# A message-passing layer on one core: the edge stage taken two groups at a time, with its PSUM banks shared out anew

## The chip, the cores and the metric

The kernel runs on one core of a Trainium2 chip. The metric is the device time of one execution in microseconds. TensorE (PE) does the matrix products and the transposes, VectorE (DVE) and ScalarE (ACT) read their results out of PSUM, GpSimd (POOL) issues the gathers, and SyncE (SP) issues most of the plain transfers. PSUM has eight banks of 2 KB a partition.

## The reference

One layer of a graph network on 6250 nodes of 128 features and 100000 edges, sorted by destination, and then a residual sum and a layer norm. Everything is float32.

```python
msg_in = concat([x[src], x[dst]], -1)                 # 100000 x 256
h = relu(msg_in @ Wm1 + bm1)                          # 256
h = relu(h @ Wm2 + bm2)                               # 256
messages = h @ Wm3 + bm3                              # 128
agg = segment_sum(messages, dst) / clip(count, 1)
upd = relu(concat([x, agg], -1) @ Wn1 + bn1) @ Wn2 + bn2
out = layernorm(x + (x + upd))
```

## The kernel before

**Tables.** The first product is taken on the nodes instead of on the edges: a table `atab` holds x @ Wm1[:128] (float32), a table `btab` holds x @ Wm1[128:] split into three bfloat16 terms. An edge's first layer is then one row of `atab` by its source plus one row of `btab` by its destination. The third product is moved behind the sum over edges.

**Groups.** The edges are taken in 196 groups of 512 (`NG`, `GE`; the last group is half filled), each of four tiles of 128 edges (`GT`). Because edges are sorted by destination, a tile's destinations lie in a window of at most 21 nodes (`WB`; a dynamic loop behind the main one, empty for these inputs, takes what lies further).

**A group's way.** `fetch` gathers four times 128 rows of `atab` by an indirect DMA from POOL (L431) and copies four windows of `btab` by plain DMAs from SP (L437), into one of four buffers `rows`. `hot` makes one-hot matrices of the destinations on DVE (L452, L455). `first_layer` transposes the gathered rows on PE (L468, 16 products) and adds the `btab` terms by one-hot products (L474, 8 products of bfloat16) into `ph`, two banks, of which there is one; ACT takes the two relu out of it (L478). `second_layer` multiplies by Wm2 (L487, 16 products as the profile counts them) into two tiles `ph2` of one bank each, and DVE takes the bias and the relu out (L489). `sums` multiplies by a one-hot matrix to sum over a window's edges (L495, 8 products of 32 columns, four beside each other in the array) into `pg`, one bank, and ACT copies it out as `part` (L502). `add_up` transposes `part` on PE (L511, 6 products) into `pt`, two banks, and DVE adds its four windows to `acc` in SBUF (L516), at columns whose numbers DVE loads into registers (`load_bases`, L519).

**PSUM.** `p1` has `ph` (2 banks), `p2` two `ph2` (2), `pa` the `pg` (1), `ptp` the `pt` (2): seven banks.

**Order.** The stages of several groups are interleaved by hand. PE's order is fixed by a manual schedule. An iteration of the main loop gives PE

```python
sums(g-3); add_up(g-4) transposes; first_layer(g); second_layer(g-1)
```

The fetch of group g+2 is issued in the same iteration. The orders of DVE and ACT are by hand in the first six iterations and at the end, and are the scheduler's in between. Each of the first two groups has one node block's x @ Wn1 (`x_part`) with it; two more such blocks stand at the end of the loop. Every eighth iteration `double` loads a block of x, doubles it on DVE and stores it for the node stage.

**Before and after.** Ahead of the loop stands the making of the tables, behind it the node stage (L678 on): the third product, the node network and the norm.

Of the kernel before, what the change touches and what calls it, by code (L numbers as in the profile page):

```python
# [19 lines left out]
P = 128  # L20
# [7 lines left out]
def kernel(  # L28
# [109 lines left out]
    w1 = const.tile([P, 2, H], F32, name="w1")  # L138
# [12 lines left out]
    with tc.tile_pool(name="prep", bufs=1) as prep, tc.tile_pool(  # L151
# [3 lines left out]
    ) as pb:  # L155
        src_i = prep.tile([R, 2 * GE], I32, name="src_i", tag="src_i")
# [256 lines left out]
    with edge, tc.tile_pool(name="wk", bufs=2) as wk, tc.tile_pool(  # L413
        name="p1", bufs=1, space=PSUM
    ) as p1, tc.tile_pool(name="p2", bufs=2, space=PSUM) as p2, tc.tile_pool(
        name="pa", bufs=1, space=PSUM
    ) as pa, tc.tile_pool(name="pt", bufs=1, space=PSUM) as ptp:


        NH2 = 4  # L420
# [4 lines left out]
        def fetch(idx, nt, firsts):  # L425


            rows = ld.tile([P, (GT + 1) * H], F32, name="rows", bufs=4)
            ag = rows[:, :GT * H].rearrange("p (j h) -> p j h", j=GT)
            for j in range(GT):  # L430
                nc.gpsimd.indirect_dma_start(  # L431
                    out=ag[:, j, :], out_offset=None, in_=atab[:, :],
                    in_offset=bass.IndirectOffsetOnAxis(ap=idx[:, j:j + 1], axis=0))
            bw = rows[:, GT * H:].bitcast(BF16).rearrange("p (k h) -> p k h", k=2)
            for j, first in enumerate(firsts):
                terms = btab[ds(first, WB + 1)].rearrange("n c h -> (n c) h")
                nc.sync.dma_start(bw[j // 2 * NQ:(j // 2 + 1) * NQ, j % 2, :], terms[:NQ])  # L437
            return ag, bw
# [7 lines left out]
        def hot(db, pb_cols, dl, nt):  # L446


            n = nt * WN
            oht = wk.tile([P, 2, P], BF16, name="oht")  # L450
            for k in range(2):
                nc.vector.tensor_scalar(oht[:n, k, :], db[:n, k * P:(k + 1) * P], pb_cols[:n, k:k + 1], None,  # L452
                                        op0=ALU.is_equal)
            oh = wk.tile([P, GT, WN], F32, name="oh", bufs=4)
            nc.vector.tensor_tensor(oh[:, :nt, :], iota_n.to_broadcast([P, nt, WN]),  # L455
                                    dl.rearrange("p (j o) -> p j o", o=1).to_broadcast([P, nt, WN]),
                                    op=ALU.is_equal)
            return oht, oh
# [3 lines left out]
        def first_layer(ag, bw, oht, nt):  # L462
            nh = nt // 2
            ph = p1.tile([P, 2, HC, 2 * P], F32, name="ph")
            for c in range(HC):
                for u in range(GT):
                    for h in range(nh):
                        nc.tensor.matmul(ph[:, h, c, u * NQ:(u + 1) * NQ], ag[halves[h], u, c * P:(c + 1) * P],  # L468
                                         ident[halves[h], halves[h]], is_transpose=True,
                                         start=(c == 0 and u == 0), stop=False, skip_group_check=True)  # L470
            for c in range(HC):
                for k in range(2):
                    for h in range(nh):
                        nc.tensor.matmul(ph[:, h, c, k * P:(k + 1) * P], bw[halves[h], k, c * P:(c + 1) * P],  # L474
                                         oht[halves[h], k, :], start=False, stop=True, skip_group_check=True)
            h1 = wk.tile([P, HC, GE], F32, name="h1")
            for c in range(HC):
                nc.scalar.activation(h1[:, c, :nh * 2 * P].rearrange("p (h e) -> p h e", h=nh), ph[:, :nh, c, :],  # L478
                                     AF.Relu, bias=b1[:, c:c + 1])
            return h1  # L480

        def second_layer(h1, h2, nt):
            for j0 in range(0, nt, 2):
                ph2 = p2.tile([P, 2, H], F32, name="ph2")
                for a in range(2):
                    for c in range(HC):
                        nc.tensor.matmul(ph2[:, a, :], h1[:, c, (j0 + a) * P:(j0 + a + 1) * P],  # L487
                                         w2[:, c, :], start=(c == 0), stop=(c == HC - 1))
                nc.vector.tensor_tensor(h2[:, j0:j0 + 2, :H], ph2, nb2.to_broadcast([P, 2, H]), op=ALU.max)  # L489

        def sums(oh, h2, nt):

            pg = pa.tile([P, H + 1], F32, name="pg")
            for j in range(nt):
                nc.tensor.matmul(pg[j * WN:(j + 1) * WN, :], oh[:, j, :], h2[:, j, :],  # L495
                                 start=True, stop=True, skip_group_check=True)
            return pg

        def part_of(pg, nt):
            n = nt * WN  # L500
            part = wk.tile([P, H + 1], F32, name="part")
            nc.scalar.copy(part[:n, :], pg[:n, :])  # L502
            return part

        def add_up(part, firsts, nt):
            pt = ptp.tile([P, 2, 4 * P], F32, name="pt")[:, :, :(HC + 1) * NQ]
            pt = pt.rearrange("p h (c q) -> p h c q", q=NQ)
            for c in range(HC + 1):
                for h in range(nt // 2):
                    rows = part[halves[h], c * P:(c + 1) * P] if c < HC else part[halves[h], H:].to_broadcast([NQ, P])  # L510
                    nc.tensor.matmul(pt[:, h, c, :], rows, ident[halves[h], halves[h]], is_transpose=True,  # L511
                                     start=True, stop=True, skip_group_check=True)
            for j in reversed(range(nt)):
                window = acc[:, :, ds(firsts[j], WB)]
                k = j % 2 * WN
                nc.vector.tensor_add(window, window, pt[:, j // 2, :, k:k + WB])  # L516
# [28 lines left out]
        def bank_p1():  # L545
            return p1.tile([P, 2, HC, 2 * P], F32, name="ph")[:, 0]

        def bank_p2():
            return p2.tile([P, 2, H], F32, name="ph2")

        ahead, lag = 2, 3
        st, hots = {}, {}
        first = list(X_FIRST)
        for i in range(NG + ahead + 1):
            if i == 6:
                turns.close()
            if i == 16:
                late_loads()

                none = wk.tile([16, (NG * GE - E) // 16 + 1], I32, name="none", bufs=1)  # L560
                nc.vector.memset(none, NONE)
                nc.sync.dma_start(dpad[E - 16:].rearrange("(p e) -> p e", p=16), none)
                nc.sync.dma_start(dpad[:E].rearrange("(p e) -> p e", p=16), dst.rearrange("(p e) -> p e", p=16))
            for step, after in enumerate((20, 24, 27)):
                if i >= after and (i - after) % 8 == 0 and (i - after) // 8 < len(pieces):
                    double((i - after) // 8, step)
            if i < NG:
                nt = GT if i < NGF else LT
                firsts = load_bases(tilei[0:1, i * GT:(i + 1) * GT], nt, ENG.SP)
                if i == NGF:  # L570
                    dbs = last_destinations()
                elif i % 2 == 0:
                    dbs = early.pop(0) if early else destinations(i, min(2, NGF - i), dst_row)
                st[i] = dict(nt=nt, got=fetch(srcT[:, i, :], nt, firsts), db=dbs.pop(0))
            g = i - ahead
            if 0 <= g < NG:
                s = st[g]
                ag, bw = s.pop("got")

                def make_hot(g):  # L580
                    s = st[g]
                    hots[g], s["oh"] = hot(s.pop("db"), pbase[:, g, :], dloc[:, g, :s["nt"]], s["nt"])

                if g not in hots:
                    make_hot(g)
                oht = hots.pop(g)
            k = g - lag
            pg = sums(st[k]["oh"], st[k]["h2"], st[k]["nt"]) if 0 <= k < NG else None
            k = g - lag - 1
            if 0 <= k < NG:  # L590
                s = st.pop(k)
                if "firsts" not in s:
                    s["firsts"] = load_bases(tilei[0:1, k * GT:(k + 1) * GT], s["nt"], ENG.DVE)
                add_up(s["part"], s["firsts"], s["nt"])
            if 0 <= g < NG:
                s = st[g]
                s["h1"] = first_layer(ag, bw, oht, s["nt"])
            if pg is not None:
                st[g - lag]["part"] = part_of(pg, st[g - lag]["nt"])
# [220 lines left out]
```

## Time and profile before

| | |
|---|---|
| median of three runs | 1203.84 us (1203.38 to 1206.65) |
| the profiled execution | 1204.24 us |
| its span, first to last instruction | 1202.5 us |
| PE busy | 1180.1 us, 98% |
| PE weight loads busy | 896.9 us, 75% |
| POOL busy | 801.2 us, 67% |
| DVE busy | 675.7 us, 56% |
| ACT busy | 419.2 us, 35% |
| granted PE clock | 0.996 |
| gathers (L431) | 784, 955 ns each |

The profiled execution lies 0.4 us above the median, and its time is 1.7 us longer than its span. In the profile's rows a matmul's duration counts from its start to the end of its last result, so that the durations of neighbours overlap; what a stage takes is read from the start of its first product to the start of the next stage's first product.

### The profile page before, as it was taken

Reading aid. Unit: us, or ns where it says so; the run is one execution under the profiler, and the core shown is the slowest. Engines: PE = TensorE matmul, PEld = TensorE weight load, DVE = VectorE, ACT = ScalarE, POOL = GpSimd, SP = SyncE. Lnnn points to the kernel's source line nnn. Section 1 sums busy time; section 2 is a strip of 40 time slices with the busy share of each in tenths; the row PEclk is TensorE's granted clock in tenths of the full one; section 3 lists DMA queues with packets and bytes.
Section 4 is the critical chain, followed back from the end, with each engine's and each line's share of the span. In section 5 each row is a group of like instructions: output and inputs, shape, how many; then the busy total and the mean of one; then the engine's idle time right before and its main releaser. Section 6 shows DMA issues by size and latency. Waiting matters only on the chain. (4 is left out here: it accounts for less than half of the span.)

```text
span 1202.5 us, 32806 instructions
## 1 busy us (share of the span) xinstructions
PE 1180.1 (98%) x11196; PEld 896.9 (75%) x11197; DVE 675.7 (56%) x2077; ACT 419.2 (35%) x776; POOL 801.2 (67%) x862
## 2 busy tenths in 40 slices
PE   8999999999999999999999999999999999999997
PEld 6747777777777777777777777777777777777565
DVE  5764555555555455555555555555555555555587
ACT  5753332332332333233233323323323332332256
POOL 6567777777777777777777777777777777773120
PEclk9999999999999999999999999999999999999998
DMA  8886666676555555555555555555555555552243
GB/s 274 280 264 191 183 194 185 182 193 185 160 151 153 150 148 153 152 151 152 152 149 147 153 153 152 153 150 149 148 154 154 150 152 151 147 147 67 83 117 114
DMA packets 173733, 193.66 MB, mean 161 GB/s; under 512 B 30906, under 2 KB 145548, under 8 KB 173548
## 3 DMA queue, kind: packets, MB, share of 16 engines
q0 software_dynamic: 38160, 103.75, 31.5%
q1 hardware_dynamic: 106956, 61.93, 17.7%
q10 hardware_dynamic: 28448, 25.87, 7.3%
q8 instruction: 89, 1.46, 0.5%
q14 instruction: 80, 0.66, 0.2%
HBM read 168.92 MB, written 22.88 MB: 160 GB/s over the span
## 5 line engine op out<-in xcount | busy, mean ns | idle before, releaser
L431 POOL DMA_INDIRECT rows<-atab,srcT x784 | 749.0, 955 | 285.4 <-issue 181.0
L487 PE MATMUL ph<-w,h 128*128 128x256 f32 x3128 | 727.6, 386 | 0.1
L487 PEld LDWEIGHTS ph<-w,h 128*128 128x128 f32 x3128 | 579.0, 190 | 91.1 <-ACT x_sb L329 0.9
L489 DVE TENSOR_TENSOR h<-ph,nb 128x512 f32<-128x512 f32 x391 | 270.6, 693 | 388.7 <-PE ph L487 376.4
L478 ACT ACTIVATE h<-ph,b 128x512 f32<-128x512 f32 x392 | 247.3, 682 | 138.4 <-PE ph L474 133.1
L502 ACT COPY part<-pg 128x257 f32<-128x257 f32 x196 | 73.6, 376 | 575.5 <-PE pg L495 510.6
L516 DVE TENSOR_TENSOR acc<-acc,pt 128x63 f32 x782 | 172.0, 220 | 78.1 <-PE pt L511 20.5
L468 PE MATMUL ph<-ident,rows 64*128 64x64 f32 x3128 | 129.9, 223 | 1.3 <-ACT h L478 0.7
L495 PE MATMUL pg<-h,oh 128*32 128x257 f32 x1564 | 125.6, 392 | 0.0
L468 PEld LDWEIGHTS ph<-ident,rows 64*128 64x128 f32 x3128 | 113.1, 140 | 2.3 <-ACT h L478 0.9
L511 PEld LDWEIGHTS pt<-ident,part 64*128 64x128 f32 x1173 | 51.1, 137 | 81.5 <-issue 81.1
L452 DVE TENSOR_SCALAR oht<-db,pbase 128x128 bf16<-128x128 int32 x392 | 100.9, 289 | 0.1
L495 PEld LDWEIGHTS pg<-h,oh 128*32 128x32 f32 x1564 | 30.9, 108 | 65.8 <-issue 65.0
L511 PE MATMUL pt<-ident,part 64*128 64x64 f32 x1173 | 77.8, 239 | 0.1
L474 PE MATMUL ph<-oht,rows 64*128 64x128 bf16 x1564 | 76.1, 216 | 0.9 <-DMA rows<-btab 0.8
L701 POOL TENSOR_TENSOR agg<-total,rc 128x512 f32<-128x512 f32 (+2 forms) x15 | 16.0, 1069 | 69.5 <-DMA rcol<-acc 33.2
L455 DVE TENSOR_TENSOR oh<-iota_n,dloc 128x128 f32<-128x128 f32 x196 | 55.9, 285 | 0.0
L474 PEld LDWEIGHTS <-rows 64*128 64x128 bf16 x1564 | 53.2, 96 | 1.4 <-DMA rows<-btab 0.9
L235 PE MATMUL pbt<-w,xT 128*128 128x256 f32 x196 | 49.8, 398 | 3.9 <-DVE rest L255 1.2
L235 PEld LDWEIGHTS pbt<-w,xT 128*128 128x128 f32 x196 | 36.6, 198 | 13.4 <-DVE rest L255 2.9
L724 PEld LDWEIGHTS pot<-wu,u 128*128 128x128 f32 (+1 forms) x196 | 24.0, 191 | 5.1 <-issue 4.5
L696 PE MATMUL pmt<-acc,w 128*128 128x512 f32 (+2 forms) x60 | 24.8, 551 | 2.3 <-DVE rc L690 2.3
(111 smaller groups left out, 410.7 us busy)
## 6 DMA issues: line engine op xcount, KB each, us to landing
rows<-btab SPq DMA_DIRECT2D x782, 32.0 KB
db<-in_dst_dram ACTq DMA_DIRECT2D x194, 128.0 KB
rows<-atab,srcT POOLq DMA_INDIRECT x784
btab<-bt SPq DMA_DIRECT2D x24, 384.0 KB
atab<-bt SPq DMA_DIRECT2D x24, 256.0 KB
xd<-in_x_dram SPq DMA_DIRECT2D x12, 256.0 KB
x2tab<-xd SPq DMA_DIRECT2D x12, 256.0 KB
x_sb<-in_x_dram SPq DMA_DIRECT2D x5, 512.0 KB
```

The costliest lines, as they stand in the source:

```text
L235: nc.tensor.matmul(pbt[:, a, :], xT[:, (t0 + a) * P:(t0 + a + 1) * P], w1[:, k, :], start=True, stop=True)
L431: nc.gpsimd.indirect_dma_start(out=ag[:, j, :], out_offset=None, in_=atab[:, :], in_offset=bass.IndirectOffsetOnAxis(ap=idx[:, j:j + 1], a ...
L452: nc.vector.tensor_scalar(oht[:n, k, :], db[:n, k * P:(k + 1) * P], pb_cols[:n, k:k + 1], None, op0=ALU.is_equal)
L468: nc.tensor.matmul(ph[:, h, c, u * NQ:(u + 1) * NQ], ag[halves[h], u, c * P:(c + 1) * P], ident[halves[h], halves[h]], is_transpose=True, ...
L474: nc.tensor.matmul(ph[:, h, c, k * P:(k + 1) * P], bw[halves[h], k, c * P:(c + 1) * P], oht[halves[h], k, :], start=False, stop=True, skip ...
L478: nc.scalar.activation(h1[:, c, :nh * 2 * P].rearrange("p (h e) -> p h e", h=nh), ph[:, :nh, c, :], AF.Relu, bias=b1[:, c:c + 1])
L487: nc.tensor.matmul(ph2[:, a, :], h1[:, c, (j0 + a) * P:(j0 + a + 1) * P], w2[:, c, :], start=(c == 0), stop=(c == HC - 1))
L489: nc.vector.tensor_tensor(h2[:, j0:j0 + 2, :H], ph2, nb2.to_broadcast([P, 2, H]), op=ALU.max)
L495: nc.tensor.matmul(pg[j * WN:(j + 1) * WN, :], oh[:, j, :], h2[:, j, :], start=True, stop=True, skip_group_check=True)
L502: nc.scalar.copy(part[:n, :], pg[:n, :])
L511: nc.tensor.matmul(pt[:, h, c, :], rows, ident[halves[h], halves[h]], is_transpose=True, start=True, stop=True, skip_group_check=True)
L516: nc.vector.tensor_add(window, window, pt[:, j // 2, :, k:k + WB])
```

## The change

Every step of the edge stage takes a pair of groups in place of one: 98 iterations in place of 196.

- `first_layer` does the 32 transposes of both groups, then the 16 one-hot products of both; `ph` has four banks.
- `sums` stands behind the one-hot products, no longer at the head of the iteration, and sums both groups into a tile of two banks. PE's order in an iteration is now: the 12 transposes of `turned` (pair p-3), `first_layer` (pair p), `sums` (pair p-2), `second_layer` (pair p-1, first and second group).
- The results of `sums`, of `turned` and of the two `second_layer` calls, and of the `x_part` calls in the loop and behind it, all take turns in one pool of two tiles of two banks each (`banks`).
- `second_layer` takes a group's result out in one DVE instruction of 1024 columns for the first group and in two of 512 for the second (`cuts`).
- `part_of` copies both groups' sums in one ACT instruction.
- `rows` has two buffers, each for a pair. `h2s` has two tiles in place of four, `h1` is twice as large, `w1` moves into a pool that is closed after the tables.
- The loads of a pair's window columns on DVE stand ahead of its eight additions, and DVE's and ACT's orders are by hand throughout.

```diff
-        NH2 = 4
+        NH2 = 2
+        def banks():
+            return p2.tile([P, 2, 2 * H], F32, name="banks")
...
-            rows = ld.tile([P, (GT + 1) * H], F32, name="rows", bufs=4)
+            rows = ld.tile([P, 2, (GT + 1) * H], F32, name="rows", bufs=2)
...
-                oh = wk.tile([P, GT, WN], F32, name="oh", bufs=4)
+                oh = wk.tile([P, GT, WN], F32, name="oh", bufs=6)
...
-            ph = p1.tile([P, 2, HC, 2 * P], F32, name="ph")
+            ph = p1.tile([P, 2, 2, HC, 2 * P], F32, name="ph")
+            for i, ((ag, bw), nt) in enumerate(zip(got, nts)):
...
+            for i in reversed(range(len(nts))):
...
-        def second_layer(h1, h2, nt):
-            for j0 in range(0, nt, 2):
-                ph2 = p2.tile([P, 2, H], F32, name="ph2")
+        def second_layer(h1, h2, nt, cuts):
+            ph2 = banks().rearrange("p b (t h) -> p (b t) h", t=2)
             for j in range(nt):
+                for c in range(HC):
+                    nc.tensor.matmul(ph2[:, j, :], h1[:, c, j * P:(j + 1) * P],
+                                     w2[:, c, :], start=(c == 0), stop=(c == HC - 1))
+            step = nt // cuts
+            for j in range(0, nt, step):
+                nc.vector.tensor_tensor(h2[:, j:j + step, :H], ph2[:, j:j + step],
+                                        nb2.to_broadcast([P, step, H]), op=ALU.max)
+        def sums(groups):
+            pg = banks()
...
+        def turned(part, nts):
+            pt = banks()[:, :, :2 * (HC + 1) * NQ].rearrange("p h (g c q) -> p h g c q", g=2, q=NQ)
...
+        def add_up(pt, firsts, nts):
+            for i in reversed(range(len(nts))):
+                for j in reversed(range(nts[i])):
+                    window = acc[:, :, ds(firsts[i][j], WB)]
+                    k = j % 2 * WN
+                    nc.vector.tensor_add(window, window, pt[:, j // 2, i, :, k:k + WB])
+                    yield
...
+        for i in range(NP + 4):
...
+            if i < NP:
...
+            p = i - 1
+            k = p - 3
+            firsts = bases(k, ENG.DVE) if k >= 0 else None
+            if k >= 0:
+                pt = turned(st[k]["part"], st[k]["nts"])
+                whole(add_up(pt, firsts, st.pop(k)["nts"]))
...
+            if p + 1 < NP:
+                make_hot(p + 1)
+            if p < NP:
+                s["h1"] = first_layer(s.pop("got"), s.pop("ohts"), s["nts"])
+            if p < 2:
+                whole(x_part(X_FIRST[p], bank, (nc.scalar, nc.vector)))
+            if p - 2 == NP - 1:
+                whole(rest)
+            if 0 <= p - 2 < NP:
+                st[p - 2]["part"] = part_of(summed(p - 2), st[p - 2]["nts"])
+            if 0 <= p - 1 < NP:
+                for j, nt in enumerate(s["nts"]):
+                    second_layer(s["h1"][:, j], h2s[j], nt, 1 + j)
```

## The prediction

> **What bounds the kernel now.** I read the page first. PE is busy in 98% of the span, and the page's 40 slices show it at 9 tenths from the second to the last but one. So only less PE time, or a wait that displaces it, can move the end. A busy PE is not a PE at its peak, so I then read PE's timeline over one group in mid-run, where the stages repeat every 5.27 us:
>
> ```profile
> 604.79 0.64 PE L495 MATMUL pg<-h,oh 128*32 128x257 f32 x8
> 605.36 0.40 PE L511 MATMUL pt<-ident,part 64*128 64x64 f32 x6
> 605.60 0.66 PE L468 MATMUL ph<-ident,rows 64*128 64x64 f32 x16
> 606.10 0.39 PE L474 MATMUL ph<-oht,rows 64*128 64x128 bf16 x8
> 606.41 3.72 PE L487 MATMUL ph<-w,h 128*128 128x256 f32 x16
> 610.06 0.64 PE L495 MATMUL pg<-h,oh 128*32 128x257 f32 x8
> ...
> 147.63 2.64 PE L487 MATMUL ph<-w,h 128*128 128x256 f32 x11
> ```
>
> Columns: start, length, then the group. The starts give what each stage takes to the next one's first product: sums 0.57, turned sums 0.24, transposes 0.50, one-hot 0.31, second layer 3.65. The last line, cut off by the end of the query, gives the pace inside a stage: five products more (3.72 against 2.64) cost 1.08, 0.216 each. Sixteen at that pace are 3.46, so 0.19 of the 3.65 is paid once per visit. The tile view shows where half of it is: the first product runs 0.10 longer than the others (maximum against median):
>
> ```profile
> L487 PE MATMUL ph<-w,h x20: 378/379/483, 603.8 to 609.8; 128*128 128x256 f32 x20
> ```
>
> The same reading elsewhere: transposes (0.66 - 0.223)/7 = 0.062 a pair of products, eight pairs 0.50, nothing paid at entry; turned sums, three pairs 0.19, so 0.05 paid; one-hot (0.39 - 0.216)/3 = 0.057 a pair, four pairs 0.23, so 0.08 paid; sums, two rounds of four beside each other, 0.43, so 0.14 paid. **A group pays 0.19 + 0.05 + 0.08 + 0.14 = 0.47 us for entering and leaving stages.** No idle row shows it.
>
> Next, the timeline of the other engines, for what lies closest behind PE:
>
> ```profile
> 604.90 0.69 DVE L489 TENSOR_TENSOR h<-ph,nb 128x512 f32<-128x512 f32 x1 [1.03 <-PE ph L487]
> 605.51 0.28 DVE L455 TENSOR_TENSOR oh<-iota_n,dloc 128x128 f32<-128x128 f32 x1
> 606.12 0.98 DVE L516 TENSOR_TENSOR acc<-acc,pt 128x63 f32 x4 [0.33 <-issue]
> 606.59 1.26 ACT L478 ACTIVATE h<-ph,b 128x512 f32<-128x512 f32 x2 [0.66 <-PE ph L474]
> ...
> 98.84 0.95 POOL L431 DMA_INDIRECT rows<-atab,srcT  x1 [0.30 <-PE ph L487]
> 100.10 1.12 POOL L431 DMA_INDIRECT rows<-atab,srcT  x1 [0.30 <-issue]
> ```
>
> POOL's gathers follow each other at 1.257 us (98.84 to 100.10) when nothing holds them: 5.03 a group, only 0.24 below PE's 5.27. **POOL is the wall behind PE.**
>
> **The change part by part.** *Fewer stage visits.* A pair visits each stage once, so the 0.47 is paid once and not twice: the products of a pair take 2 x 5.27 - 0.47 = 10.08 us in place of 10.55. Here a rule bears: the Trainium skill's "TensorEngine Tiling (Array Packing)", Key Properties, says that a changed tiling mode drains TensorE, and "TensorE: Matmul & The Clock Gate", step by step, puts a drain at some 128 cycles, an estimated 0.05 us at its 2.4 GHz. A pair has three changes of tile shape fewer (64x128 to 128x128, to 128x32, back), so the rule's sum is 0.16 a pair, 15 us in all; the trace's is 0.47, 44 us. The trace has both sides of the gap, the drain and the first weights' load that nothing hides (the 0.10 above), so I take the trace.
>
> *Sums moved behind the one-hot products.* Sixteen products, same count. They wait for the last relu of the pair's second layer on DVE (over 0.8 us after that layer's end, by the L489 rows: last product at 604.49, DVE 604.90 to 605.59); sums come 1.95 into the iteration. Hidden.
>
> *Two tiles of two banks for all.* Turn by turn, `pt` and the first `ph2` share one, `pg` and the second `ph2` the other. So the first `second_layer` of an iteration waits for the eight additions on DVE, which had banks of their own. Count from the iteration's first product. PE wants that tile at 0.05 + 6 x 0.062 + 16 x 0.062 + 8 x 0.057 + 0.08 + 4 x 0.216 + 0.14, which is 2.96. DVE ends the last relu of the layer before at 0.80. The column load started as soon as the instruction ahead of it had gone out, and the additions 0.61 after that (605.51 to 606.12); a second load for the second group, 0.34 more, is an estimate from the length of such a load in the trace. Counted from the last relu's start (0.11), the first addition is at 1.06, the eighth seven steps of 0.255 later, its end at 3.07, PE's release some 0.06 after: 3.13. **PE stands 0.17 us in every pair.** A bound below: if both loads are hidden, additions start at 0.80 and end at 2.81, no wait. Above: if a load costs twice that, 0.5. A rule speaks against the change here: "Perfetto Trace Analysis", Optimizing Tensor Performance, wants independent products to rotate through different PSUM banks, so that one's reading overlaps the next one's writing. By the rows its price is the 0.17; without the rows it could be the whole of the additions. The second `ph2` wants its tile at 6.5 and gets it from ACT: four relus at 0.59 from 2.1 and a copy, done by 5.3. Hidden; without that cover it would be 0.7.
>
> *One relu of 1024 columns.* By the slope of two rows (128x256 0.41, 128x512 0.68) 1.2 us, beside the second group's 3.46 us of products. `ph` of four banks: read by 4.6, wanted at 10.5. Hidden.
>
> *Fetching by pairs.* Eight gathers, 10.06 us, against 10.25 of PE: POOL stays ahead by a hair. A pair's buffer is free after its one-hot products, at 1.9; its gathers end about 12 later and are wanted at 20.7, so no wait. SP's eight copies take some 6.3 (28 of them 22.4 us in its timeline), hidden.
>
> *Moved orders on DVE and ACT.* Behind the additions DVE has one-hots of 1.5 us (wanted 5 us later), and ACT issues the destinations' two transfers ahead of the relus, after a copy that ended 5 us earlier. `double`, 0.7 us every fourth pair, follows the additions. None reaches PE.
>
> **Start and end.** Pairs lose at both ends, and these are worked out in absolute time. The first one-hot products waited for SP:
>
> ```profile
> 80.92 22.40 SPq L437 DMA_DIRECT2D rows<-btab  x28
> 85.60 0.34 PE L474 MATMUL ph<-oht,rows 64*128 64x128 bf16 x5 [0.79 <-DMA rows<-btab]
> ...
> 1125.88 0.69 ACT L329 ACTIVATE xT<-ph,bu 128x512 f32<-128x512 f32 x1 [1.22 <-PE ph L327]
> 1127.47 0.42 DVE L690 TENSOR_SCALAR rc<-acc 128x106 f32<-128x106 f32 x2 [2.54 <-ACTq L635]
> ```
>
> SP needs about 3.1 us a group, so group 1's windows are there at 88.3 and group 3's at 94.4, where PE formerly had second-layer work in between. One-hot of pair 0 ends at 88.4, a node block to 90.5, pair 1 at 94.4, a block, second layer of pair 0 to 102.2, pair 2 and second layer of pair 1 to 112.1. So iteration 3 starts at 112.2; the same work stood some 2.5 us further in the old order. From there 95 iterations at 10.25 end at 1086. The next has no first layer to hide the additions: 0.43 turned, sums, then a wait until 3.1, 24 products: 8.5. The last: node blocks in turn through two tiles, each waiting for ACT's 0.69, then sums, two copies, nine transposes, six additions: 9.6. Work ends at 1104.1, and the node stage starts 0.9 behind the last ACT row, as it did (1126.57 to 1127.47): 1105.0, in place of 1127.47.
>
> **The sum.** 94 iterations save 0.30 each (0.47 - 0.17), 28 us; start and end give 6 back: 22.5 us. The span 1202.5 becomes 1180.0, the execution 1204.24 becomes 1181.7, and against the median, 0.4 lower, **1181 us**.
>
> **The rivals.**
> - *No wait for the additions.* For it: the loads ran beside another DVE instruction in the trace, so the second may be hidden too. Against: it is in DVE's queue ahead of the additions. Then 10.08 a pair: 95 x 0.17 = 16 us less, 1165. Chance 0.2.
> - *POOL becomes the bound.* For: 0.24 of slack a group; after a wait its gap is 0.55 and not 0.30. Against: it waits only when ahead. With 0.25 once a pair, 10.06 becomes 10.31 and the time 1187. Chance 0.1.
> - *The shared tiles hand over late* (the other side). If the first `ph2` waits not for the additions but for ACT's copy of `pg`, at 5.3, PE stands 2.3 us a pair: 95 x 2.3 = 219 us, less the 44 saved and plus the 6, about 1385. For it: two tiles for four results, and nothing in the trace of before shows their turn. Against: the order of use pairs `pt` with the first `ph2`. A milder form is additions that start late. Slower begins where the wait is over 0.41 a pair (the 0.17 plus 22.5/95), additions ending at 3.4 and not 3.07. Chance, both forms, 0.11.
> - *The cost is not per visit* but per product: nothing is saved, start and end cost 6, and the wait is covered: 1210. Against: the first product alone is longer. Chance 0.03.
>
> **How the numbers follow.** My case has 0.56. 0.3% is 3.6 us, about what a measurement of this kernel can tell from no change. A wait near 0.4 a pair ends within that: 0.02 of my case and 0.02 of the late hand-over, 0.04. Slower is what is left of the late hand-over and the last rival, 0.12; faster 0.54 + 0.2 + 0.1 = 0.84. The range runs from the first rival less 2 (no loss at the start), 1163, to a wait of 0.38, 1201; that leaves out the slower cases and little below.
>
> **What would show it.** Right: one L487 row of 32 products, about 7.0 us, per iteration, iterations about 10.25 apart, and a gap of 0.1 to 0.2 ahead of it released by DVE L516. POOL's longest waits again name PE. Wrong: the gap names ACT L502 or passes 0.4; the first product's 0.10 turns up in the middle of a stage; PE waits for gathers at L468; or the node stage starts later than 1127.

## The result, and the profile after

The changed kernel takes 1215.57 us (median of four runs, 1213.36 to 1215.88), the kernel before 1203.83 in the same study: a ratio of 1.0089, 95% interval 1.0069 to 1.0108. It is slower by 11.7 us, where 22.5 us less was forecast. In three further studies the kernel before itself took 1401 to 1425 us and every kernel with pairs 1.18 to 1.46 times as long, at a granted clock of 0.81 to 0.88 against its 0.99, for a cause that is not known; their times are given below as set aside, and each of these kernels was run again.

The profiled execution took 1215.59 us, its span 1213.9. The page first:

```profile
PE 1139.8 (94%) x11196; PEld 909.9 (75%) x11197; DVE 651.5 (54%) x1978; ACT 381.9 (31%) x679; POOL 803.9 (66%) x862
...
L499 PE MATMUL banks<-w,h 128*128 128x256 f32 x3128 | 698.6, 381 | 45.8 <-DVE acc L542 43.0
```

PE's busy time fell by 40 us (1180.1 before) in a span that grew by 11: PE has less to do, and stands idle more. The second layer's products last 381 ns in the mean (386 before: the longer first product came once in 16 then, and comes once in 32 now). The last column has the idle time ahead of them and what ended it: 43.0 us were ended by the additions, where the same column held 0.1 us in all before.

The timeline over one pair, PE's rows first, then DVE's of the same stretch:

```profile
608.97 0.58 PE L533 MATMUL banks<-ident,part 64*128 64x64 f32 x12
609.39 1.16 PE L478 MATMUL ph<-ident,rows 64*128 64x64 f32 x32
610.38 0.61 PE L485 MATMUL ph<-oht,rows 64*128 64x128 bf16 x16
610.92 1.07 PE L511 MATMUL banks<-h,oh 128*32 128x257 f32 x16
612.42 7.14 PE L499 MATMUL banks<-w,h 128*128 128x256 f32 x32 [0.43 <-DVE acc L542]
619.50 0.58 PE L533 MATMUL banks<-ident,part 64*128 64x64 f32 x12
...
609.08 1.29 DVE L503 TENSOR_TENSOR h<-banks,nb 128x512 f32<-128x512 f32 x2 [2.23 <-PE banks L499]
610.28 2.00 DVE L542 TENSOR_TENSOR acc<-acc,banks 128x63 f32 x8
```

From start to start, over the 85 pairs between 150 and 1050 us whose rows are complete, the medians are: turned sums 0.415, transposes 0.996, one-hot 0.540, sums 1.50, second layer 7.076, in all 10.53 a pair against twice 5.273 before. Four of the five are the shortened stages that were foreseen. Only sums are too long: sixteen products at 0.216 and 0.14 for the entry are 1.00, so 0.50 of the 1.50 is the wait for the tile. Take it out, and a pair is 10.03.

DVE's first row is the one that decides. The two relus of the second group both run after 609.08, though the first of them reads results that PE had finished some 1.7 us earlier (the eight products behind them, at 0.216 each). They end at 610.37, 1.40 after the iteration's first product. The additions follow them, and the tile comes free 3.31 after the start; PE's next product in it starts at 3.45.

The list of waits (total, times, longest) has the same:

```profile
POOL rows L437 <- PE ph L485: 59.6, 80, 1.0
...
PE banks L499 <- DVE acc L542: 43.0, 94, 0.9
```

PE's wait comes 94 times in 98 iterations: it isn't an accident of the ends. POOL still waits for PE, so it is not the wall.

### The profile page after: what moved, and what is told of

The parts are those of the page before. It is cut to its first block, busy times and chain, and to the rows that moved or that the text cites. A ratio compares the mean times of both kernels' runs of the same rounds, so it can differ in the third digit from the quotient of the medians.

```text
span 1213.9 us, 31892 instructions
## 1 busy us (share of the span) xinstructions
PE 1139.8 (94%) x11196; PEld 909.9 (75%) x11197; DVE 651.5 (54%) x1978; ACT 381.9 (31%) x679; POOL 803.9 (66%) x862
## 3 DMA queue, kind: packets, MB, share of 16 engines
q8 instruction: 89, 1.46, 0.5%
## 5 line engine op out<-in xcount | busy, mean ns | idle before, releaser
L499 PE MATMUL banks<-w,h 128*128 128x256 f32 x3128 | 698.6, 381 | 45.8 <-DVE acc L542 43.0
L499 PEld LDWEIGHTS banks<-w,h 128*128 128x128 f32 x3128 | 586.2, 190 | 165.8 <-PE banks L511 86.2
L503 DVE TENSOR_TENSOR h<-banks,nb 128x512 f32<-128x512 f32 (+1 forms) x294 | 245.7, 864 | 477.3 <-PE banks L499 471.4
L542 DVE TENSOR_TENSOR acc<-acc,banks 128x63 f32 x782 | 171.6, 219 | 31.8 <-PE banks L533 5.8
L478 PE MATMUL ph<-ident,rows 64*128 64x64 f32 x3128 | 113.8, 223 | 0.6 <-issue 0.6
L511 PE MATMUL banks<-h,oh 128*32 128x257 f32 x1564 | 105.3, 386 | 1.0 <-DVE acc L542 1.0
L533 PEld LDWEIGHTS banks<-ident,part 64*128 64x128 f32 x1173 | 43.3, 137 | 33.2 <-issue 31.8
L511 PEld LDWEIGHTS banks<-h,oh 128*32 128x32 f32 x1564 | 40.9, 109 | 28.8 <-PE banks L533 1.1
L519 ACT COPY part<-banks 128x514 f32<-128x514 f32 x97 | 58.6, 604 | 9.9 <-PE banks L511 9.9
L533 PE MATMUL banks<-ident,part 64*128 64x64 f32 x1173 | 56.7, 229 | 0.5 <-ACT part L522 0.5
```

The costliest lines, as they stand in the source:

```text
L478: nc.tensor.matmul(ph[:, i, h, c, u * NQ:(u + 1) * NQ], ag[halves[h], u, c * P:(c + 1) * P], ident[halves[h], halves[h]], is_transpose=Tru ...
L499: nc.tensor.matmul(ph2[:, j, :], h1[:, c, j * P:(j + 1) * P], w2[:, c, :], start=(c == 0), stop=(c == HC - 1))
L503: nc.vector.tensor_tensor(h2[:, j:j + step, :H], ph2[:, j:j + step], nb2.to_broadcast([P, step, H]), op=ALU.max)
L511: nc.tensor.matmul(pg[j * WN:(j + 1) * WN, i, :H + 1], oh[:, j, :], h2[:, j, :], start=True, stop=True, skip_group_check=True)
L519: nc.scalar.copy(part[:, :n], pg[:, :n, :H + 1])
L533: nc.tensor.matmul(pt[:, h, i, c, :], rows, ident[halves[h], halves[h]], is_transpose=True, start=True, stop=True, skip_group_check=True)
```

## The experiments

The theory that came out of the trace (*whole tile*, theory H in the earlier expectations): a reader of a PSUM tile waits for the tile's last product, so both relus of the second group start behind the layer; that makes the additions late, and the additions make the second layer late. Its rivals: the two column loads, which stand in DVE's queue ahead of the additions and end level with the relus, hold them; or the wait is not on the path, and the pairs lose their time elsewhere.

### Half of the additions left out

```diff
-                whole(add_up(pt, firsts, st.pop(k)["nts"]))
+                steps = add_up(pt, firsts, st.pop(k)["nts"])
+                for _ in range(4):
+                    next(steps)
```

Four of a pair's eight additions are left out, so that half of the windows' sums are missing. It was run three times; the first two are set aside (1651.04 and 1657.87 us):

> The changed kernel with four of the eight additions of every pair left out (those of its first group, so that half the sums are missing); all else as it was. A dose for the hand-over: additions end at 2.3 in place of 3.3. Theory H: the shared tile is free at 2.4, before PE's 2.95, no wait, iterations 10.03 to 10.08, 1167 to 1173 us. Rival V: the additions are beside PE's work and their number does nothing, 1213 to 1216 us.

> The kernel of e4 once more: four of the eight additions of a pair left out, half the sums missing. Theory H: additions end at 2.3, no wait, iterations 10.03 to 10.08, 1167 to 1173 us. Rival V (their number does nothing): 1213 to 1216 us.

> The kernel of e9 once more, for the same reason: four of the eight additions of a pair left out, half the sums missing. Theory H: additions end at 2.3, no wait, iterations 10.03 to 10.08, 1167 to 1173 us. Rival V (their number does nothing): 1213 to 1216 us.

The third took 1167.04 us (1166.3 to 1168.09), ratio 0.9687 (0.9662 to 0.9711), 48.5 us below the changed kernel. Its timeline:

```profile
604.79 0.58 PE L533 MATMUL banks<-ident,part 64*128 64x64 f32 x12
...
606.74 1.07 PE L511 MATMUL banks<-h,oh 128*32 128x257 f32 x16
607.75 6.53 PE L499 MATMUL banks<-w,h 128*128 128x256 f32 x29
...
604.90 1.29 DVE L503 TENSOR_TENSOR h<-banks,nb 128x512 f32<-128x512 f32 x2 [2.23 <-PE banks L499]
606.11 0.98 DVE L542 TENSOR_TENSOR acc<-acc,banks 128x63 f32 x4
```

The additions start as late as in the changed kernel (1.32 after the first product), but end 1.0 earlier, at 2.30. The second layer starts at 2.96 with no wait in its row, which is the 2.96 that the prediction worked out for PE's want. The sums' stage is 1.004, an iteration 10.06. So the wait is on the path, and its 0.50 a pair is worth all of the loss and all of the gain that was missed.

### The column loads alone

```diff
-            firsts = bases(k, ENG.DVE) if k >= 0 else None
...
+            if 0 <= p - 2 < NP:
+                ahead[p - 2] = bases(p - 2, ENG.DVE)
             if 0 <= p - 1 < NP:
                 s = st[p - 1]
                 for j, nt in enumerate(s["nts"]):
                     second_layer(s["h1"][:, j], h2s[j], nt, 1 + j)
```

The loads are issued on DVE ahead of the relus of the iteration before. The first three runs are set aside (1698.13, 1690.0 and 1780.11 us).

> The changed kernel with the two column loads of the next pair placed on DVE ahead of the second layer's relus instead of behind them. Theory H: the relus still end at 1.40, additions start at 1.3, no gain: 1212 to 1216 us. Rival L (the loads alone hold the additions): the additions start some 0.5 earlier and the wait goes, 1170 us.

> The kernel of e2 once more: the changed kernel with only the column loads ahead of the second layer's relus. Theory H: the relus alone still let the first addition start at 1.29 after the iteration's first product, in place of 1.31; iteration 10.5, 1212 to 1215 us. Rival L (the loads alone hold the additions): 1170 us.

> Only the two column loads of the additions are moved, ahead of the second layer of the iteration before. Whole tile theory: the last two relus start behind the tile's last product and end 1.40 us after the iteration's start, level with the loads, so without the loads the additions start no earlier than some 1.3 us: iteration 10.5 to 10.56 us, 1209 to 1216 us. Rival, the loads hold the additions: they start at 0.7 to 0.8 us, the wait ahead of the second layer falls by some 0.5 to nothing, iteration 10.06 us, about 1168 us.

> As before: the two column loads of the additions are moved ahead of the second layer of the iteration before, and nothing else. Whole tile theory: the last two relus end 1.40 us after the iteration's start all the same, the additions start no earlier than some 1.3 us: iteration 10.5 to 10.56 us, 1209 to 1216 us. Rival, the loads hold the additions: they start at 0.7 to 0.8 us, iteration 10.06 us, about 1168 us.

The fourth took 1211.48 us (1210.81 to 1212.4), ratio 1.0056 (1.0037 to 1.0075). The timeline, PE and then DVE:

```profile
606.77 0.58 PE L533 MATMUL banks<-ident,part 64*128 64x64 f32 x12
...
610.23 7.14 PE L499 MATMUL banks<-w,h 128*128 128x256 f32 x32 [0.43 <-DVE acc L542]
...
606.88 1.29 DVE L503 TENSOR_TENSOR h<-banks,nb 128x512 f32<-128x512 f32 x2 [2.23 <-PE banks L499]
608.09 2.00 DVE L542 TENSOR_TENSOR acc<-acc,banks 128x63 f32 x8
```

With no load between them and the relus, the additions start 1.32 after the first product, as before, and the wait is 0.43, as before; the five stages have the same medians to 0.001 us. The 4 us by which this kernel is faster lie mostly at the ends: iteration 3 starts 1.7 us earlier, and the last stretch before the node stage is 2.0 us shorter. The loads hide behind the relus. The rival falls: while the relus are as late as here, they alone hold the additions.

### Products and relus alternating in one tile

```diff
-            for j in range(nt):
-                for c in range(HC):
-                    nc.tensor.matmul(ph2[:, j, :], ...)
             step = nt // cuts
-            for j in range(0, nt, step):
-                nc.vector.tensor_tensor(h2[:, j:j + step, :H], ph2[:, j:j + step], ...)
+            for j0 in range(0, nt, step):
+                for j in range(j0, j0 + step):
+                    for c in range(HC):
+                        nc.tensor.matmul(ph2[:, j, :], ...)
+                nc.vector.tensor_tensor(h2[:, j0:j0 + step, :H], ph2[:, j0:j0 + step], ...)
```

The first relu of the second group is written between the two halves of its products, so that it waits for its own half. It was run alone and together with the early loads; the first run of each is set aside (2039.56 and 2036.53 us).

> The changed kernel with the second group's products and relus interleaved: two tiles' products, their relu, two tiles' products, their relu. In the trace of the changed kernel both relus of that group start only behind its last product (609.08 and 609.68, the layer's end being 608.97). Theory H (the hand-over of the shared tile sets the wait of 0.47 us a pair, and the additions' start is held by two things that are level: the relus, done at 1.40, and the two column loads, which started with the first relu and let the first addition go 1.19 after): taking the relu away alone leaves the loads, which then start with the last relu at 0.12, so the first addition is at 1.3 as before; 1213 to 1216 us, iteration 10.53. Rival R (the relus alone hold the additions): they start 0.6 earlier, the wait is gone, 1170 us, iteration 10.05.

> The kernel of e1 once more, for the same reason. Theory H: the loads still hold the additions, 1213 to 1216 us, iteration 10.53. Rival R (the relus alone hold them): 1170 us.

> Both edits together. Theory H: last relu from 0.11, additions from 0.8 to 2.8, release at 2.9, level with PE's 2.95: the wait is under 0.05 us, iterations 10.03 to 10.08, 95 of them save 0.45 to 0.5 each, 1168 to 1173 us. Rival P (GpSimd's gathers take over with 10.06 and 0.25 for a wait once a pair): iterations 10.3, 1193 us. Rival V (the cost is not per visit of a stage, and PE's time comes back elsewhere): 1205 us or more.

> The kernel of e3 once more: in that study the kernel before itself took 1401 us[...], and TensorE stood for microseconds in every iteration where no row names a cause. Where the kernel before takes its 1204 us, theory H says: no wait for the additions, iterations 10.03 to 10.08, 1168 to 1173 us; rival P (gathers take over) 1193 us; rival V (the cost is not per visit of a stage) 1205 us or more.

The relu alone: 1302.78 us, ratio 1.0825 (1.0807 to 1.0843). With the loads: 1268.17 us, ratio 1.0529 (1.0512 to 1.0547). Both missed what the theory expected of the total. By its number alone, 1268 us is what the last rival expected (1205 us or more, PE's time coming back elsewhere); the timeline of the kernel with both moves shows where it comes back:

```profile
603.04 1.99 PE L501 MATMUL banks<-w,h 128*128 128x256 f32 x8 [0.78 <-DVE h L503]
604.97 0.58 PE L533 MATMUL banks<-ident,part 64*128 64x64 f32 x12
...
607.92 5.45 PE L501 MATMUL banks<-w,h 128*128 128x256 f32 x24
...
602.30 0.69 DVE L503 TENSOR_TENSOR h<-banks,nb 128x512 f32<-128x512 f32 x1 [0.50 <-PE banks L501]
605.08 0.69 DVE L503 TENSOR_TENSOR h<-banks,nb 128x512 f32<-128x512 f32 x1 [2.08 <-PE banks L501]
605.68 2.00 DVE L542 TENSOR_TENSOR acc<-acc,banks 128x63 f32 x8
```

The additions do what the theory asked for: one relu runs early, only one stands behind the layer, and they start 0.71 after the iteration's first product and end at 2.71; the second layer starts at 2.95 with no wait. But PE's first row is new: the later half of the products now waits for the relu of the earlier half, 0.78 us in mid-layer, though it writes to the other bank of the tile. The layer takes 8.157, where it takes 7.105 in the kernel with half of the additions, which has no wait ahead of it either. So the order within a tile holds both ways: a reader stands behind all products written before it, a product behind all readers written before it. What the one wait gave (0.50), the other took twice over (1.05).

With the relu alone early, the loads do bind:

```profile
607.74 0.58 PE L533 MATMUL banks<-ident,part 64*128 64x64 f32 x12
...
608.89 2.01 DVE L542 TENSOR_TENSOR acc<-acc,banks 128x63 f32 x8 [0.36 <-DVE h L503]
...
611.05 5.42 PE L501 MATMUL banks<-w,h 128*128 128x256 f32 x24 [0.28 <-PE banks L511]
```

The additions start at 1.15 (and DVE stands 0.36 ahead of them), and 0.36 of wait is left in the sums' stage (1.361 against 1.004). PE's row names its own sums, but its product starts 0.15 after the last addition ends (611.05 and 610.90), as in the changed kernel. So the late relus had covered loads that would have delayed the additions to 1.16 in any case (the median), and only 0.14 of the 0.50 goes with the relus alone: the prediction's 1.06 for the loads was 0.10 short.

### Tiles of one bank

```diff
-        def banks():
-            return p2.tile([P, 2, 2 * H], F32, name="banks")
+        def bank(k=0):
+            return p2.tile([P, 2, H], F32, name=f"bank{k}", tag=f"bank{k}")
...
+            for j0 in range(0, nt, 2):
+                ph2 = bank(cuts - 1)
...
+            pt = [bank().rearrange(...)[...] for h in range(2)]
...
+            for h in reversed(range(2)):
+                for i in reversed(range(len(nts))):
+                    for j in (2 * h + 1, 2 * h):
```

The same four banks and the same order of stages, but in four tiles of one bank, two in turn for each of two uses: `ph2` is a tile per two edge tiles with a relu of its own, as in the kernel before, and `pt` and `pg` are two tiles each. So each relu waits for its own eight products, and the first `ph2` waits for four of the additions, not for eight. The first run is set aside (1666.11 us, a ratio of 1.1878).

> The changed kernel with the shared tiles cut into tiles of one bank: the turned sums are two tiles, each read by four of the additions (first those of one, then those of the other), the sums of the two groups two tiles, and the second layer four tiles of two products each with a relu of 512 columns for each. Turned sums and the first group's second layer share two banks, sums and the second group's share the other two. No relu waits for products of another tile, and no product for a relu of another tile. Theory H: the first half of the additions is over at 2.3, before PE wants the bank at 2.95, the second half at 3.3, before 3.9; no wait, iterations 10.03 to 10.08, 1167 to 1173 us. Rival P (gathers take over): iterations 10.3, 1193 us. Rival V (the cost is not per visit of a stage): 1205 us or more.

> The kernel of e7 once more, since in that study the kernel before took 1402 us, with TensorE standing in the middle of stages where no row names a cause. Where the kernel before takes its 1204 us, theory H says: no wait for the additions, iterations 10.03 to 10.08, 1167 to 1173 us. Rival P (gathers take over): iterations 10.3, 1193 us. Rival V (the cost is not per visit of a stage): 1205 us or more.

The second took **1167.65 us** (1165.49 to 1169.53), ratio 0.9685 (0.966 to 0.971): below both kernels. Its timeline (PE, DVE, POOL) and one row of its waits:

```profile
608.23 0.58 PE L527 MATMUL bank<-ident,part 64*128 64x64 f32 x12
...
611.19 1.13 PE L497 MATMUL bank<-w,h 128*128 128x256 f32 x4
...
606.61 0.69 DVE L499 TENSOR_TENSOR h<-bank,nb 128x512 f32<-128x512 f32 x1 [1.03 <-PE bank L497]
608.34 0.69 DVE L499 TENSOR_TENSOR h<-bank,nb 128x512 f32<-128x512 f32 x1 [1.03 <-PE bank L497]
609.39 2.01 DVE L539 TENSOR_TENSOR acc<-acc,bank 128x63 f32 x8 [0.36 <-DVE h L499]
...
610.07 0.95 POOL L434 DMA_INDIRECT rows<-atab,srcT  x1 [0.31 <-DMA xd<-in_x_dram]
611.33 0.95 POOL L434 DMA_INDIRECT rows<-atab,srcT  x1 [0.30 <-issue]
...
POOL rows L434 <- issue: 207.9, 682, 0.3
```

(The row of L497 with four products is cut off by the end of the query.) One relu stands beside the products of the other half, the last ends 0.80 after the first product of the iteration (608.34 and 0.69, against 608.23), and the second layer starts at 2.96 with no wait. The additions, held by the loads at 1.16, end at 3.17, later than 2.96, and it doesn't matter, because only four of them stand ahead of the first tile: in the trace PE's queue passes its wait on DVE at 610.42, as the fourth addition ends, and has a second wait ahead of the next tile. So the edit does two things at once, and no run parts them. By the rows, the relus' own tiles bring the additions from 1.31 to 1.16, and the division of `pt`, with the additions in the order of its two tiles, does the rest: with all eight additions ahead of it, the first `ph2` would not be free before 3.17. The late relu's wait belonged to the tile, as the program is built, and not to the bank: in the changed kernel the first of the two reads one bank and waited for products that write the other. An iteration is 10.06. That is also eight gathers at 1.26 (610.07 to 611.33), and POOL's gathers in the loop stand no more than some 0.3 apart: POOL and PE are level, and by these rows a shorter PE alone would gain nothing more here.

### The sums moved alone

```diff
-            k = g - lag
-            pg = sums(st[k]["oh"], st[k]["h2"], st[k]["nt"]) if 0 <= k < NG else None
...
+            k = g - lag
+            pg = sums(st[k]["oh"], st[k]["h2"], st[k]["nt"]) if 0 <= k < NG else None
```

The kernel before, with the sums behind the one-hot products; one group at a time, all banks as they were. The first two runs are set aside (1401.63 and 1431.29 us, ratios 0.9999, from 0.9990 to 1.0008, and 1.0049, from 1.0024 to 1.0074).

> The kernel before with one part of the change alone: sums behind the first layer's one-hot products, groups still taken singly and the PSUM layout as it was. Theory H (a stage's entry costs per visit, and the number of visits is the same): 1202 to 1207 us. Rival O (the order itself, bfloat16 products next to sums in place of next to the second layer, is what changes the entry costs): more than 5 us either way.

> The kernel before with one thing changed: the sums stand behind the one-hot products. The same four stages a group are entered in another order, so that the changes of tile shape stay as many (64x128 to 128x32 to 128x128 in place of 128x128 to 128x32 to 64x64). Theory that what is saved is the visits and not the order: a group stays at 5.25 to 5.30 us, the time within 0.5% of before. Rival, the order itself saves: a group at 5.15 us or less, 1180 us or less.

> As before: the kernel before with the sums behind the one-hot products and nothing else. Visits and changes of tile shape stay as many. Theory that the visits carry what the stages saved: a group stays at 5.25 to 5.30 us, the time within 0.5% of before. Rival, the order itself saves: a group at 5.15 us or less, 1180 us or less.

The third took 1206.03 us (twelve runs), ratio 1.0007 (0.9998 to 1.0016); a group is 5.271 us. So the order of the stages carries nothing. What is left for the 0.5 us a pair that the stages lost is that they are entered half as often; no run changes that alone, but the saving lies stage by stage where it was worked out (below).

## Why the prediction was wrong, point by point

**The saving per visit: right.** Foreseen were 10.08 us a pair without a wait; the changed kernel shows 10.03 beside its wait, and the two kernels without one show 10.06, so 0.49 is saved where 0.47 was worked out. It lies where it was put: against twice the stages of before, the kernel with half of the additions saves 0.06 in turned sums, nothing in transposes, 0.09 in one-hot, 0.14 in sums and 0.20 in the second layer (worked out: 0.05, 0, 0.08, 0.14, 0.19). Its total was right too: the rival with no wait was put at 1165 us, and the two kernels in which the wait is gone take 1167.0 and 1167.7. Here the rows were weighed against the rule of the Trainium skill ("TensorEngine Tiling (Array Packing)", Key Properties) that a change of tiling mode drains TensorE, with 0.47 against an estimated 0.16 a pair from the drain of some 128 cycles that "TensorE: Matmul & The Clock Gate" (Step-by-step) gives. The rows hold: 0.49 is three times the estimate, and the one-hot stage pays its 0.09 although its tile shape is that of the transposes before it (64*128 in both rows). How the price divides between a drain and a first weights' load that nothing hides, no run here shows.

**The wait: the mechanism right, the size wrong, and this is the step that failed.** The prediction named the right tile, the right releaser and the right moment of PE's want (2.96, seen in two kernels). The sum that put the end of the additions at 3.07 and the wait at 0.17 failed; the additions end at 3.31, and 0.50 was measured. Three of its terms were too small.

- "DVE ends the last relu of the layer before at 0.80": it ends at 1.40. The term was read off the kernel before, where each `ph2` is a tile for two edge tiles and the first relu runs beside the later products. In the change a group is one tile, and both relus start behind its last product. The additions start at 1.31, which is 0.15 later than the loads alone let them start in the two kernels with an early last relu (1.16).
- "a second load for the second group, 0.34 more": the second load starts 0.42 after the first (609.09 and 609.51 in the trace), and the loads alone make the first addition start at 1.16 and not at 1.06, which is 0.10.
- "PE's release some 0.06 after": from the last addition to PE's product it is 0.14 (612.28 to 612.42), which is 0.08.

With the 0.17 these make 0.50. So the late relus are the largest of three terms and not the whole. In the kernel with the relu alone early, whose last relu ends at 0.80 as foreseen, 0.36 of the wait is left; an estimate from this, 0.14 less in each of 94 pairs, puts the changed kernel at some 1202 us, still without a gain worth the name. The prediction's bound above, 0.5 "if a load costs twice that", met the size by luck: no load cost twice as much.

**What the miss of 34 us is made of.** The span is 33.9 us longer than foreseen. The start was nearly right: iteration 3 starts at 112.86, and 112.2 was worked out, 0.7 us. From iteration 3 to iteration 97, 10.56 each was measured and 10.25 foreseen: 94 times 0.31, 29 us. The tail took 3 us more:

```profile
1105.50 0.58 PE L533 MATMUL banks<-ident,part 64*128 64x64 f32 x12
...
1110.14 7.17 PE L499 MATMUL banks<-w,h 128*128 128x256 f32 x32 [1.62 <-ACT part L519]
1117.24 0.57 PE L533 MATMUL banks<-ident,part 64*128 64x64 f32 x12
...
1125.99 0.58 PE L533 MATMUL banks<-ident,part 64*128 64x64 f32 x12
...
1136.24 0.47 DVE L542 TENSOR_TENSOR acc<-acc,banks 128x63 f32 x2 [0.28 <-DVE acc L542]
...
1138.89 0.42 DVE L697 TENSOR_SCALAR rc<-acc 128x106 f32<-128x106 f32 x2 [2.18 <-issue]
```

Iteration 97 is 11.74 long, the next 8.75 (foreseen 8.5), the last 10.7 until its additions end (foreseen 9.6). In iteration 97 the wait is put down to ACT's copy, and is 1.2 longer than elsewhere. The kernel with the early loads waits 0.43 at the same place and the one with half of the additions not at all, neither for ACT; why the changed kernel does stays open. The node stage starts 2.2 after the last addition (1136.71 to 1138.89), where 0.9 was put behind the end of the work, 1.3 more, and then takes 75.0 as before.

**The rivals.** That the shared tiles hand over late is what happened, in the milder form: additions that start late. "Slower begins where the wait is over 0.41 a pair" was right: it was 0.50, and the kernel is slower. The point given beside it, additions ending at 3.4, does not follow from its own terms: 3.07 and 0.24 make 3.31, and with the measured hand-over it is 3.23. The 3.31 that was measured lies on the wrong side of that. The form that has ACT's copy hold the first `ph2` in every pair did not come. POOL is not the bound of the changed kernel. It becomes level with PE at 10.06 when the wait is gone, and the 10.31 of that rival did not come.

**The rule that spoke against the change.** The page "Perfetto Trace Analysis" (Optimizing Tensor Performance) of the Trainium skill wants independent products to rotate through different PSUM banks. By the rows it was weighed at 0.17. It cost 0.50, and the runs show what the rotation needs here. The products of a layer did go through different banks in the changed kernel; but two banks in one tile are one thing to wait for, and the same banks in tiles of their own bring the time from 1215.6 to 1167.7.

**What would show it.** The mark set for wrong was a gap that passes 0.4; the rows say 0.43, by DVE L542. The mark was well placed; the chance of 0.11 for it was too small, because the start of the relus was taken over from a kernel whose tiles were cut otherwise, without asking what a relu waits for when its tile is larger, and because the second load and the hand-over were taken at their least.

## What to carry to other kernels

When results are put together in a larger PSUM tile, read again every wait on that tile, in both directions: its first reader now starts behind its last product, and its next writer behind its last reader. The relu's duration could be carried over from the old trace (0.69 in both); its start could not, because it belonged to the old tile. Entering a stage has a price (here 0.47 us for four stages) that no idle row shows, and larger batches save it; to keep the saving here, it was enough to batch the order of the products and leave the tiles at one bank.

## What the runs showed of the hardware that was not expected

- Where a relu in the same tile stood between two halves of a layer, PE stood 0.78 us for it, although the halves lie in different banks, and the first weights of the next half came 1.19 after the last ones. The layer lost 1.05 us (8.157 against 7.105), more than the relu's 0.69.
- From the last addition to PE's next product in its tile it took 0.14 us, where 0.06 had been put: the addition ends at 612.28, the first weights' load starts at 612.39, the product at 612.42.
- The second layer takes 7.105 us without a wait ahead of it and 7.076 behind one, so that 0.03 of a wait comes back. POOL is not the reason, though eight gathers at 1.257 us also are 10.06: in the two kernels with the early relu, whose iterations of 11.1 and 11.4 are too long for POOL to bound them, the layer shows the same (8.157 without a wait, 8.129 behind one). Behind the wait the first weights' load starts 0.03 ahead of the first product (612.39 and 612.42); in the kernel before, which has no wait there, both start at 606.41.
